# Four source blocks in one weight tile, bounds taken from exponentials, and a re-ranked instruction list in a four-layer graph network

## The chip, the cores and the metric

The kernel runs on one NeuronCore of a Trainium2 chip. The metric is device time in microseconds (us) of one execution, as a median of several executions; less is better. The engines are named as in the profile: PE is TensorE (matmuls), PEld its weight loads, DVE is VectorE, ACT is ScalarE, POOL is GpSimd, SP is SyncE, which here only issues DMAs. L1083 means line 1083 of the kernel before.

## The reference: what is computed

Sixteen graphs (B = 16) of N = 1024 nodes with D = 256 features each pass through four layers. Each layer is `x = x + layer(relu(layernorm(x)), adj)`; `adj` is a symmetric 0/1 matrix with ones on its diagonal.

```
layer 0: relu(h @ W_upd + (adj^T @ (h @ W_msg)) / degree + bias)
layer 1: 4 heads of 64: softmax over neighbours of leaky_relu(e_src_i + e_dst_j, 0.01),
         weighted sum of h @ W, + bias, relu, + h @ W, layernorm over the head's 64 features
layer 2: 4 heads of 64: the same attention with slope 0.2, weighted sum, then elu
layer 3: 1 head of 256: the same attention with slope 0.2, weighted sum
```

## The kernel before, in words

**Mathematics.** Everything is in float32. The exponential of a leaky ReLU of a sum is factored: up to a factor that cancels in the softmax, the weight of source j for target i is `max(exp((1-slope)*s_i), exp(-(1-slope)*e_j)) * mask[j, i]`, and the other factor `exp(e_j)` is multiplied into the features. So one DVE instruction makes the weights of 128 sources: `masked` (L1077 to L1090; the instruction is L1083) takes `max` of a row `r` (the same in all partitions) and a per-partition scalar `tt`, times the mask. PE then multiplies these weights with the features. A guard at the end compares bounds of the exponents (tile `mx`) with a limit; a general program would run if they were exceeded, which these inputs do not bring about.

**Per graph.** `layer0` normalises and transposes `x` (`norm_t`), projects it (L1112 to L1129: split in two float32r parts), and gathers over the adjacency (L1143, L1146; PE alone is busy, 64 pairs of matmuls). `heads` is run for layers 1 and 2: normalise, `project_all` (L984 on PE, L1003 on ACT), `terms`, and then for each of four heads eight source blocks `jb`, each one `masked` of 128x1024 on DVE and one `product` on PE (L1266, 32 records in the trace), and an epilogue mostly on DVE. `layer3` does the same for one head of 256 features in four groups `i2` of 256 targets: eight `masked` of 128x256 and eight `product` (L1420, 4 records each) a group, then a reciprocal (L1434), two final additions (L1445) and the store.

**Terms.** `terms` (L1014) makes for each attention layer: `es` = exp of the source term (ACT, L1024), its transpose (PE, L1034), a copy `r4` to SBUF (ACT, L1038), a write to DRAM (`rd`, L1042) and, by `spread`, a broadcast read into `r` (L1067). `bounds` (DVE, L1050 to L1052) takes three maxima of the raw terms from the projected tile `wh`; after it, because it overwrites these terms, `raise_t` (ACT, L1057 and L1058) makes `tt` and raises the target terms in place. `weigh` (DVE, L1247) or, in layer 3, eight ACT scalings (L1407) then multiply features with the raised terms.

**Buffers.** Every tile has a tag with so many buffers (`BUFS`). Tag `p` has six tiles of 128x1024 float32: each head weight block takes one, each layer-3 weight block takes one too and uses 256 of its 1024 columns, and `r4` takes one as well. Tag `acc` (two PSUM tiles) holds the sums of a head or group.

**What sets the order.** The engines run lists that a planner, class `Plan`, writes at build time. `do` records an operation with its engine, an estimated cost and its dependences, and a priority: the PE time of the graph's earlier operations (`plan.pos`), plus the graph's offset `b * SHIFT` (38.75 us apart), plus a per-stage and per-engine `RANK`, plus `slack`. `emit` repeatedly takes, among all ready operations, the one that can start earliest; ties in that time go to the lower priority number. Each engine executes its list in that order, so an instruction that waits holds what stands behind it on the same engine. A gate keeps the operations of graph b + 2 out of the list until the first operation of layer 3 of graph b, so at most about two graphs are under way.

Of the kernel before, what the change touches and what calls it, by code (L numbers as in the profile page):

```python
# [8 lines left out]
F32 = mybir.dt.float32  # L9
# [9 lines left out]
P = 128  # L19
# [7 lines left out]
SHIFT = 38.75  # L27

ENGINES = ("pe", "dve", "act", "pool", "sp")
RANK = {  # L30
    "load": (-255, -45, -146, -223, -161),
    "setup": (147, 44, -129, 45, 72),
    "norm0": (132, -159, -111, 18, -3),
    "split0": (-94, 119, -51, -165, -111),
    "mask": (77, 143, 41, 193, 218),
    "gather0": (241, -7, 71, 23, 10),
    "norm1": (-60, -62, -162, -146, -99),
    "project1": (20, 26, -5, 26, -6),
    "weights1": (-164, 7, -45, 57, -13),
    "heads1": (-192, -212, -213, -62, -111),  # L40
    "last1": (-26, -102, 9, -196, -80),
    "norm2": (-206, -157, 81, 6, -21),
    "project2": (79, -60, -360, 87, -40),
    "weights2": (94, -3, 153, -153, 12),
    "heads2": (-112, -33, -288, -105, -59),
    "last2": (-21, -230, -230, -36, -82),
    "norm3": (-477, -373, -518, -355, -261),
    "project3": (148, 162, -14, -78, 0),
    "weights3": (170, 143, 167, 44, 87),
    "last3": (43, -259, -75, -14, -59),  # L50
# [4 lines left out]
    "mv": 4, "st": 2, "rstd": 4, "shift": 4, "tt": 3, "es": 2, "dg": 2, "rden": 2, "sth": 1, "mh": 2, "rsh": 2,  # L55
# [16 lines left out]
class Plan:  # L72
# [8 lines left out]
    def __init__(self):  # L81
        self.ops, self.pos, self.gate, self.stage = [], 0.0, None, None

    def do(self, eng, cost, fn, r=(), w=(), lag=0.0, slack=0.0, kind="f", dma=0.0):
# [24 lines left out]
        deps.discard(k)  # L109
        self.ops.append((eng, cost, lag, fn, deps, bufs, self.pos + slack + RANK[self.stage][ENGINES.index(eng)], kind, dma))  # L110
# [3 lines left out]
    def emit(self):  # L114
# [14 lines left out]
        while ready:  # L129
            best = None  # L130
            for k in ready:
# [19 lines left out]
                if at is not None and (best is None or (at, prio, k) < best):  # L151
                    best = (at, prio, k)
            at, _, k = best
# [445 lines left out]
def tile_factored(  # L599
# [56 lines left out]
    mx = const.tile([P, B * 9], F32, name="f_mx")  # L656
    rdn = const.tile([P, B * NB], F32, name="f_rdn")
# [351 lines left out]
    def terms(wh, nh, slope, ecol, scol, k):  # L1009


        tt = buf(small, "tt", [P, NB, nh])
        r4 = buf(work, "p", [P, N])
        rd = buf(dram, "rd", [nh, N])  # L1014

        def ed():
# [3 lines left out]
        es = buf(small, "es", [P, nh, NB])  # L1020
# [4 lines left out]
                es.t, wh.t[:, :, scol : scol + nh].rearrange("p n h -> p h n"), AF.Exp, scale=1.0 - slope  # L1025
            ),
            r=[(wh, ib) for ib in range(NB)],
            w=[es],
# [5 lines left out]
            lambda: nc.tensor.transpose(pt.t[:m, :P], es.t.rearrange("p h n -> p (h n)"), ident),  # L1034
            r=[es],
# [12 lines left out]
        def bounds():  # L1048
            es = wh.t[:, :, scol : scol + nh]
            nc.vector.tensor_reduce(mx[:, k : k + 1], ed(), AX.XY, ALU.max)  # L1050
            nc.vector.tensor_reduce(mx[:, k + 1 : k + 2], ed(), AX.XY, ALU.min, negate=True)
            nc.vector.tensor_reduce(mx[:, k + 2 : k + 3], es, AX.XY, ALU.max)  # L1052

        do("dve", 0.4, bounds, r=[wh])

        def raise_t():
            nc.scalar.activation(tt.t, ed(), AF.Exp, scale=-(1.0 - slope))  # L1057
            nc.scalar.activation(ed(), ed(), AF.Exp)  # L1058

        do("act", 0.5, raise_t, w=[tt, wh])  # L1060
# [14 lines left out]
        return tt, spread  # L1075

    def masked(r, tt, mask, jb, h, lo, hi):  # L1077

        w = buf(work, "p", [P, N])
        do(  # L1080
            "dve",
            (hi - lo + 125) / 960.0,
            lambda: nc.vector.scalar_tensor_tensor(  # L1083
                w.t[:, : hi - lo], r.t[:, lo:hi], tt.t[:, jb, h : h + 1], mask.t[:, jb, lo:hi], op0=ALU.max, op1=ALU.mult
            ),
            r=[r, tt, mask],
            w=[w],
        )
        return w
# [143 lines left out]
    def heads(b, l, xs, mask, w, slope, epilogue, keep):  # L1233
# [19 lines left out]
        for h in range(H):  # L1253
# [22 lines left out]
            epilogue(b, h, ps, wh, xs, 8.0 if h + 1 < H else 0.0)  # L1276
# [19 lines left out]
    def epilogue1(b, h, ps, wh, xs, slack):  # L1296
# [45 lines left out]
        do("pool", 2.0, root, r=[mb], w=[rs], lag=0.9, slack=slack)  # L1342
# [53 lines left out]
    def layer3(b, xs, mask):  # L1396
# [15 lines left out]
        for i2 in range(NB // 2):  # L1412
            plan.stage = "weights3"
            ps = buf(acc_p, "acc", [P, 2, 512])
            for jb in range(NB):
                w = masked(r, tt, mask, jb, 0, i2 * 2 * P, (i2 + 1) * 2 * P)

                def product(w=w, ps=ps, jb=jb):
                    for q in range(2):
                        nc.tensor.matmul(  # L1420
                            ps.t[:, q, : D + 1],
                            w.t[:, q * P : (q + 1) * P],
                            wh.t[:, jb, : D + 1],
                            start=(jb == 0),
                            stop=(jb == NB - 1),
                        )

                do("pe", 0.87, product, r=[w, (wh, jb)], w=[ps])
# [12 lines left out]
            for q in range(2):  # L1441
                do(
                    "dve",
                    0.5,
# [26 lines left out]
    for b in range(B):  # L1471
        plan.pos, plan.gate = b * SHIFT, gates.get(b)
# [17 lines left out]
    for k, (t, most) in enumerate(((tot, 0.0), (mx, TERM_MAX), (rdn, 1e30))):  # L1490
        nc.vector.tensor_scalar(t, t, most, None, op0=ALU.is_le)
        nc.vector.tensor_reduce(m[:, k : k + 1], t, AX.X, ALU.min)
# [58 lines left out]
```

## Time and profile before

| quantity | value |
|---|---|
| median of 3 runs | 2736.85 us (2735.02 to 2740.15) |
| the profiled execution: its time, its span | 2741.27 us, 2739.4 us |
| granted TensorE clock, mean of the span | 0.972 |
| DVE busy | 2357.3 us (86% of the span) |
| ACT busy, POOL busy | 1143.5 us (42%), 878.0 us (32%) |
| POOL's accumulating DMA issue after layer 2's heads waits for DVE (`x L1216 <- DVE y L1388`) | 435.8 us in 46 waits |
| the reciprocal of the last layer-3 group of graphs 0, 13, 14, 15 begins at | 417, 2525, 2633, 2731 us |
| HBM read, written | 228.21 MB, 17.37 MB |

How to read it: "busy" of an engine is the time in which it executes; a row of the groups gives the line, the engine, the operation, the tiles and shapes, the count, the total and mean duration, and the idle time of that engine just ahead of such instructions with what ended it. A wait is read as "who waited for whom: total, times, longest". The windows list, for a stretch of the span, busy time and number of instructions of PE, PEld, DVE, ACT and POOL, then the granted clock, the DMA share and GB/s.

### The profile page before, as it was taken

To read this page: it belongs to the slowest core of one execution; us is meant where nothing else is said; L and a number is where in the kernel's file an instruction comes from. 1 tells how busy PE (TensorE), PEld (TensorE's weight loads), DVE (VectorE), ACT (ScalarE), POOL (GpSimd) and SP (SyncE) were. 2 spreads that over 40 slices of the span, in tenths; PEclk is the share of its full clock that TensorE was granted. 3 is DMA by queue.
4 is the path that set the end of the run, shared out by engine and by line. 5 is a ranking of instruction groups with operands and counts; after the bars stand their busy time and mean duration, and the time that the engine had idled before them with its cause. 6 is when DMAs were issued, how large, how long until landed. Compare 5 with 4: busy or idle time off the path is not lost. (4 is left out here: it accounts for less than half of the span.)

```text
span 2739.4 us, 92386 instructions
## 1 busy us (share of the span) xinstructions
PE 2547.4 (93%) x40667; PEld 2285.7 (83%) x40667; DVE 2357.3 (86%) x4790; ACT 1143.5 (42%) x2753; POOL 878.0 (32%) x907
## 2 busy tenths in 40 slices
PE   7867999999999999999999999999999999999786
PEld 6767798888888888889888889888888988888775
DVE  2699689898988989899898989989898898989884
ACT  4431625344353444525344452534435353453222
POOL 3332234324252332424224251422425133241210
PEclk9989999999999999999999999999999999999998
DMA  8724547356472745547255563735546263562121
GB/s 194 171 44 84 113 87 165 82 128 117 99 143 53 159 91 129 105 91 163 60 144 97 118 125 71 163 75 133 112 107 134 63 158 81 130 118 66 33 52 29
DMA packets 397318, 293.58 MB, mean 107 GB/s; under 512 B 179301, under 2 KB 345706, under 8 KB 396906
## 3 DMA queue, kind: packets, MB, share of 16 engines
q0 software_dynamic: 232992, 92.29, 24.8%
q1 hardware_dynamic: 160752, 193.05, 24.4%
q8 instruction: 321, 5.26, 0.8%
q10 hardware_dynamic: 3162, 2.24, 0.3%
q14 instruction: 91, 0.75, 0.1%
HBM read 228.21 MB, written 17.37 MB: 90 GB/s over the span
## 5 line engine op out<-in xcount | busy, mean ns | idle before, releaser
L1083 DVE SCALAR_TENSOR_TENSOR p<-r,tt,mask 128x1024 f32<-128x1024 f32 (+1 forms) x1536 | 1473.3, 1010 | 109.2 <-PE acc L1266 40.8
L1266 PE MATMUL acc<-wide,p 128*64 128x65 f32 x32768 | 1064.6, 227 | 135.7 <-DVE p L1083 129.3
L1266 PEld LDWEIGHTS acc<-wide,p 128*64 128x64 f32 x32768 | 1017.2, 141 | 204.0 <-issue 99.0
L984 PE MATMUL mm<-f_w,ht 128*128 128x264 f32 (+2 forms) x2048 | 477.0, 387 | 1.4 <-ACT ht L973 1.3
L1420 PE MATMUL acc<-wide,p 128*128 128x257 f32 x2048 | 462.2, 382 | 10.1 <-DVE p L1083 9.9
L1420 PEld LDWEIGHTS acc<-wide,p 128*128 128x128 f32 x2048 | 386.1, 191 | 68.1 <-issue 11.1
L984 PEld LDWEIGHTS mm<-f_w,ht 128*128 128x128 f32 x2048 | 384.6, 192 | 61.2 <-ACT ht L973 3.0
L954 ACT ACTIVATE hn<-x,shift,rstd 128x256 f32<-128x256 f32 x512 | 269.1, 591 | 257.5 <-DVE shift L941 157.1
L1356 ACT ACTIVATE t<-t,mh,rsh 128x64 f32<-128x64 f32 x512 | 176.7, 428 | 198.2 <-DVE mh L1346 174.3
L1143 PE MATMUL mm<-wide,adjr 128*128 128x258 f32 x1024 | 254.5, 289 | 0.0
L1146 PE MATMUL mm<-wide,adjr 128*128 128x256 f32 x1024 | 247.9, 282 | 0.0
L1003 ACT COPY wide<-mm 128x264 f32<-128x264 f32 (+1 forms) x384 | 141.3, 378 | 218.7 <-PE mm L984 216.5
L1216 POOL DMA_DIRECT2D x<-y x48 | 76.6, 1596 | 447.4 <-DVE y L1388 435.8
L934 POOL TENSOR_SCALAR rstd<-mv 128x4 f32<-128x4 f32 x128 | 60.7, 474 | 434.6 <-DVE mv L929 402.3
L1143 PEld LDWEIGHTS mm<-wide,adjr 128*128 128x128 f32 x1024 | 195.9, 191 | 1.7
L1146 PEld LDWEIGHTS mm<-wide,adjr 128*128 128x128 f32 x1024 | 194.2, 190 | 1.5
L922 DVE BATCH_NORM_STATS2 st<-x 128x6 f32<-128x256 f32 x512 | 183.2, 412 | 8.4 <-DMA x<-in_x_dram 5.6
L967 PE MATMUL mm<-f_ident,hn 128*128 128x128 f32 x1024 | 168.0, 300 | 20.2 <-ACT hn L954 17.2
L973 ACT COPY ht<-mm 128x512 f32<-128x512 f32 x256 | 137.8, 580 | 104.9 <-PE mm L967 103.9
L1157 POOL TENSOR_SCALAR dg<-f_deg 128x1 f32<-128x1 f32 x128 | 61.0, 476 | 359.7 <-ACT f_deg L1154 357.4
L967 PEld LDWEIGHTS mm<-f_ident,hn 128*128 128x128 f32 x1024 | 125.2, 151 | 50.4 <-ACT hn L954 35.5
L935 POOL TENSOR_TENSOR rstd<-rstd,f_mhalf 128x4 f32<-128x4 f32 x128 | 162.2, 1268 | 10.7
(103 smaller groups left out, 2179.3 us busy)
## 6 DMA issues: line engine op xcount, KB each, us to landing
r<-rd SPq DMA_DIRECT2D x144, 512.0 KB, 3.9
adjr<-in_adj_dram POOLq DMA_DIRECT2D x128, 512.0 KB, 4.7
nat<-in_adj_dram SPq DMA_DIRECT2D x128, 512.0 KB, 6.6
out_dram<-o SPq DMA_DIRECT2D x64, 256.0 KB, 2.8
x<-in_x_dram SPq DMA_DIRECT2D x31, 512.0 KB, 5.1
x<-t POOLq DMA_DIRECT2D x48, 256.0 KB, 5.5
x<-y POOLq DMA_DIRECT2D x48, 256.0 KB, 4.5
mask<-sq SPq DMA_TRANSPOSE x128, 4.7
```

Source lines behind the costliest of these rows:

```text
L922: lambda st=st, ib=ib, k=k: nc.vector.bn_stats(st.t[:, k, :], xs.t[:, ib, :]),
L935: nc.gpsimd.tensor_tensor(rstd.t, rstd.t, mhalf[:, :nh], op=ALU.pow)
L954: nc.scalar.activation(hn.t[:, k, :], xs.t[:, hf * nh + q, :], AF.Relu, bias=shift.t[:, q : q + 1], scale=rstd.t[:, q : q + 1],)
L967: nc.tensor.transpose(pt.t[:, k, c, :], hn.t[:, k, c * P : (c + 1) * P], ident)
L984: nc.tensor.matmul(out, ht.t[:, c, ib * P : (ib + 1) * P], w.t[:, c, lo:hi], start=(c == 0 and k == 0), stop=(c == KC - 1), skip_group_che ...
L1003: lambda ib=ib, ps=ps: nc.scalar.copy(wh.t[:, ib, :cols], ps.t[:, :cols]),
L1083: lambda: nc.vector.scalar_tensor_tensor(w.t[:, : hi - lo], r.t[:, lo:hi], tt.t[:, jb, h : h + 1], mask.t[:, jb, lo:hi], op0=ALU.max, op1= ...
L1143: nc.tensor.matmul(ps.t[:, : D + 2], a.t[:, ib, :], hi.t[:, ib, : D + 2], start=(ib == 0), stop=False)
L1146: nc.tensor.matmul(ps.t[:, :D], a.t[:, ib, :], lo.t[:, ib, :D], start=False, stop=(ib == NB - 1))
L1266: nc.tensor.matmul(ps.t[c : c + 64, g, q * E1 : (q + 1) * E1], p.t[:, i2 * 64 : (i2 + 1) * 64], xw.t[:, jb, h * E1 : (h + 1) * E1], start= ...
L1356: nc.scalar.activation(t.t[:, ib, :], t.t[:, ib, :], AF.Identity, bias=mb.t[:, 3, ib : ib + 1], scale=rs.t[:, ib : ib + 1],)
L1420: nc.tensor.matmul(ps.t[:, q, : D + 1], w.t[:, q * P : (q + 1) * P], wh.t[:, jb, : D + 1], start=(jb == 0), stop=(jb == NB - 1),)
```

## The change

1. Layer 3's weights of four source blocks share one tile of tag `p`: block `q = jb % 4` goes to columns 256q to 256q + 255, and a new tile is taken only for q = 0. The instruction's size stays 128x256, and the products read their part.
2. `es` and `tt` become one tile `et` (row 0 the source exponentials, row 1 the target ones); `r4` gets a small buffer of its own instead of one of tag `p`. `raise_t` is recorded ahead of `bounds`. `bounds` is now two reductions, of `et` and of the raised target terms, recorded after `raise_t` with a slack of 19.714; the limits are exponentials of the old limit, kept in a tile `lim` that six POOL memsets fill, and compared by one `tensor_tensor` at the end.
3. All `masked` of a graph keep their order (`row="weights"`: each depends on the one before).
4. The planner: after it has found the operation that can start earliest, it takes a better-ranked one of the same engine if that can start within `HOLD` (PE 0.1, DVE 0.25, ACT 0.45 us, POOL and SP 0). Each graph's offset is `b * 147.75 + START[b]` in place of `b * 38.75`. All `RANK` numbers are new; the slack of the first three heads' epilogues goes from 8 to 23; the estimated cost of the head norm's root goes from 2.0 (lag 0.9) to 2.6 (lag 1.2) and of the final addition from 0.5 to 0.43.

```diff
-SHIFT = 38.75
+SHIFT = 147.75
+HOLD = (0.1, 0.25, 0.45, 0.0, 0.0)
+START = (-50, 120, 90, 96, 162, 174, 157, 173, 171, 159, 102, 27, 24, -31, -99, -188)
...
-    "weights1": (-164, 7, -45, 57, -13),
+    "weights1": (-159, 14, 48, 187, 22),
...
-    "weights2": (94, -3, 153, -153, 12),
+    "weights2": (-69, -102, -110, -395, -48),
...
-    "project3": (148, 162, -14, -78, 0),
-    "weights3": (170, 143, 167, 44, 87),
-    "last3": (43, -259, -75, -14, -59),
+    "project3": (460, 307, 133, 13, 73),
+    "weights3": (381, 312, 355, -1, 200),
+    "last3": (-85, -237, -117, -157, -144),
...
+        if row is not None:
+            if row in self.rows:
+                deps.add(self.rows[row])
+            self.rows[row] = k
...
+            until = at + HOLD[ENGINES.index(self.ops[k][0])]
+            for a, p, q in could:
+                if self.ops[q][0] == self.ops[k][0] and a <= until and p < prio:
+                    at, prio, k = a, p, q
...
-        tt = buf(small, "tt", [P, NB, nh])
-        r4 = buf(work, "p", [P, N])
+        et = buf(small, "et", [P, 2, nh, NB])
+        r4 = buf(small, "r4", [P, P])
...
+        def raise_t():
+            nc.scalar.activation(et.t[:, 1], ed().rearrange("p n h -> p h n"), AF.Exp, scale=-(1.0 - slope))
+            nc.scalar.activation(ed(), ed(), AF.Exp)
+
+        do("act", 0.5, raise_t, w=[(et, 1), wh])
+
         def bounds():
-            es = wh.t[:, :, scol : scol + nh]
-            nc.vector.tensor_reduce(mx[:, k : k + 1], ed(), AX.XY, ALU.max)
-            nc.vector.tensor_reduce(mx[:, k + 1 : k + 2], ed(), AX.XY, ALU.min, negate=True)
-            nc.vector.tensor_reduce(mx[:, k + 2 : k + 3], es, AX.XY, ALU.max)
-
-        do("dve", 0.4, bounds, r=[wh])
-
-        def raise_t():
-            nc.scalar.activation(tt.t, ed(), AF.Exp, scale=-(1.0 - slope))
-            nc.scalar.activation(ed(), ed(), AF.Exp)
-
-        do("act", 0.5, raise_t, w=[tt, wh])
+            nc.vector.tensor_reduce(mx[:, k : k + 2], et.t.rearrange("p s h n -> p s (h n)"), AX.X, ALU.max)
+            nc.vector.tensor_reduce(mx[:, k + 2 : k + 3], ed(), AX.XY, ALU.max)
+
+        do("dve", 0.45, bounds, r=[et, wh], slack=19.714)
...
-        w = buf(work, "p", [P, N])
+        w = w or buf(work, "p", [P, N])
+        c = q * (hi - lo)
...
-            epilogue(b, h, ps, wh, xs, 8.0 if h + 1 < H else 0.0)
+            epilogue(b, h, ps, wh, xs, 23.0 if h + 1 < H else 0.0)
...
-                w = masked(r, tt, mask, jb, 0, i2 * 2 * P, (i2 + 1) * 2 * P)
+                q = jb % 4
+                w = masked(r, tt, mask, jb, 0, i2 * 2 * P, (i2 + 1) * 2 * P, w if q else None, q)
...
-        plan.pos, plan.gate = b * SHIFT, gates.get(b)
+        plan.rows = {}
+        plan.pos, plan.gate = b * SHIFT + START[b], gates.get(b)
```

## The prediction

> **What bounds the kernel now.** I read the busy shares, then the groups, the waits, the windows by stage, and last the timeline around the gaps of PE.
>
> ```profile
> PE 2547.4 (93%) x40667; PEld 2285.7 (83%) x40667; DVE 2357.3 (86%) x4790; ACT 1143.5 (42%) x2753; POOL 878.0 (32%) x907
> ...
> PEclk9989999999999999999999999999999999999998
> ...
> L1083 DVE SCALAR_TENSOR_TENSOR p<-r,tt,mask 128x1024 f32<-128x1024 f32 (+1 forms) x1536 | 1473.3, 1010 | 109.2 <-PE acc L1266 40.8
> L1266 PE MATMUL acc<-wide,p 128*64 128x65 f32 x32768 | 1064.6, 227 | 135.7 <-DVE p L1083 129.3
> ```
>
> PE is busy 93%, and what ends most of its idle time (129.3 of some 192 us) is DVE's weights. The change leaves PE's work as it is, so a gain can only come from PE's idle time and from the clock that is withdrawn around it. DVE, at 2357.3/16 = 147.3 us a graph, comes next.
>
> ```profile
> 110.00:313.00 203.00, 152.97 (x3271) 137.99 (x3270) 181.78 (x346) 68.14 (x167) 57.78 (x44) 0.90 0.35 70
> 313.00:417.00 104.00, 102.89 (x1415) 91.99 (x1415) 84.06 (x160) 41.55 (x100) 30.48 (x35) 1.00 0.58 120
> 417.00:2525.00 2108.00, 2034.63 (x33007) 1830.82 (x33007) 1905.12 (x3862) 926.90 (x2236) 720.25 (x728) 0.98 0.53 112
> 2525.00:2633.00 108.00, 88.57 (x1260) 79.63 (x1262) 88.17 (x195) 34.46 (x88) 22.19 (x18) 0.89 0.21 49
> 2633.00:2674.00 41.00, 35.57 (x1022) 31.81 (x1016) 39.76 (x40) 3.78 (x6) 4.72 (x3) 1.00 0.29 41
> 2674.00:2701.00 27.00, 12.49 (x55) 9.38 (x51) 7.51 (x31) 14.30 (x34) 2.53 (x4) 0.75 0.06 20
> ```
>
> Three regimes. The ramp (110 to 313 us): both first graphs are in their heads, DVE is the bound (181.78 of 203), PE lacks 50 us and the clock is 0.90, which costs about 153 x 0.10 = 15 us more: 65 us. The steady part: the last layer-3 groups of graphs 0 and 13 lie 2108 us apart, 2108/13 = 162.2 us a graph, with PE busy 2034.6/13 = 156.5. The end: 19.4 + 5.4 + 14.5 us without matmuls, then layer 3 of the last graph alone.
>
> Where do 5.7 us of PE's time go in each steady graph? One gap makes most of it, here in one graph (from the timeline: start and length in us, engine, line, tiles, count, and in brackets the idle time before it and who ended it; the last line is a window as above); 4.1 us recur in each graph:
>
> ```profile
> 1380.68 0.87 DVE L1083 SCALAR_TENSOR_TENSOR p<-r,tt,mask 128x256 f32<-128x256 f32 x2
> ...
> 1383.05 1.66 DVE L1083 SCALAR_TENSOR_TENSOR p<-r,tt,mask 128x256 f32<-128x256 f32 x4
> ...
> 1382.21 5.37 PE L1420 MATMUL acc<-wide,p 128*128 128x257 f32 x24
> ...
> 1391.70 2.00 PE L1266 MATMUL acc<-wide,p 128*64 128x65 f32 x32 [4.12 <-DVE p L1083]
> ...
> 1393.00:1398.00 5.00, 5.00 (x79) 4.55 (x77) 5.00 (x5) 3.04 (x6) 0.38 (x1) 0.57 1.05 338
> ```
>
> DVE lays in 2 + 4 = 6 layer-3 blocks, exactly the six tiles of tag `p`. PE eats them (24 records, 4 each) by 1387.6 while DVE is in an elu, an addition, norm statistics and layer-3 outputs, and then stands for 4.12 us. Afterwards the clock is 0.68 over 4 us and 0.57 over 5 us: with 1.3 and 5.0 us of PE work in them that is 0.4 + 2.15 = 2.5 us more. So the gap costs 6.6 us of 162.2.
>
> **What the Trainium skill says.** "TensorE: Matmul & The Clock Gate", the part on the HAM clock gate: after about 3.4 us of idling PE's clock is halved until about 3.4 us of work have passed. The trace agrees (0.57 after a gap of 4.12 us). The same page, on engine queue depths, has ACT and DVE as strict FIFOs; the waits below agree. "Perfetto Trace Analysis", Optimization Strategy: the same gap repeating on the engine that should be saturated can mean too few buffers for the next tile. The six blocks before that gap fit this.
>
> ```profile
> PE acc L1266 <- DVE p L1083: 129.3, 56, 8.5
> DVE f_mx L1050 <- ACT wide L1003: 111.1, 21, 11.5
> DVE p L1083 <- PE acc L1420: 35.3, 79, 4.9
> ACT wide L1058 <- DVE f_mx L1052: 30.4, 14, 2.3
> ```
>
> **The change, part by part.**
>
> *One tile for four layer-3 blocks.* The instructions and their sizes stay: 512 of 477 ns. Six tiles now hold 24 such blocks, or eight blocks (a whole group) hold two tiles and leave four to the heads. It removes the 35.3 us of DVE behind L1420, and lets DVE lay in more for PE: another six blocks are 6 x 4 x 0.226 = 5.4 us of PE work (5.37 / 24 = 0.224 a record), above the gap of 4.12. Bounds: 0 if the new list does not lay in more ahead of that stretch, 13 x 6.6 = 86 us if every gap closes. A tile is now held until its fourth product; with two tiles a group against six before I cost that at nothing, since the heads' weights gain tiles; if PE lets a quarter-used tile lie, its price is one tile of six, one head block of 1.2 us of DVE lead. `r4` outside tag `p` frees one tile from L1038 to the write of `rd` (about 2 us), 48 times; it is inside the same bound. I take half of the gap's cost, 3.5 us a graph: **13 x 3.5 = 45 us**. I chose half because the list must still place the blocks well and DVE's 147 us a graph leave little room in 156.
>
> *Bounds from exponentials.* Before: 32 x (207 + 202 + 175) + 16 x (160 + 154 + 154) ns = 18.7 + 7.5 = 26.2 us of DVE. After, two reductions: for 64 elements I estimate 0.25 us (207 ns at 32 elements, 160 at 8: 2 ns an element, so 0.21 to 0.27), and the last one stays: 32 x 0.43 + 16 x 0.32 = 18.9. So 7 us less of DVE in all, 0.5 us a graph, nothing where PE is the bound. The 111.1 us that DVE stood before L1050 are mostly under PE's projections and would be waited out at the next instruction; I count 0. L1058's 30.4 us go; what is late next is `r` (`rd` 1.7 us and the broadcast 3.7 us after it), so again 0; bounds 0 to 30/16 = 1.9 us a graph, in the half above. The new waits: in layer 2 `weigh` writes over what `bounds` reads and stands behind it on DVE itself; in layer 3 the planner puts the ACT scalings after `bounds`. Behind these scalings on ACT stand copies of projections and norms, and PE's L1420 waits for them. `bounds` has a slack of 19.7, so this may be late (rival D). Six POOL memsets at the start (0.1 us each, as L1100's 106 ns) lie before PE's first matmul at 13.7 us, which waits for a DMA: 0, or 0.6 us if uncovered. The last comparison replaces one of like width: 0 to 0.1 us.
>
> *Weights in order.* Same engine, so no wait is added; the order inside a graph was nearly this: 0, at worst a few blocks of 1.2 us in a graph.
>
> *Offsets and ranks.* At the start graph 0 now stands 318 us ahead of graph 1 in the priorities (-50 against 147.75 + 120), not 38.75. Before, the two layers 0 shared PE and DMA until 110 us, with DVE busy 31.9 of 110 us; the first head weights came at 110.1. If graph 0 goes first it needs half of that PE work (about 52 us a graph by L1143, L1146, L1182 and the projections), and can begin its heads some 20 us earlier; graph 1's layer 0 then fills PE under graph 0's heads, and graph 2 gets past its gate, the first layer-3 operation of graph 0, well before 313 us. Moved with it are graph 1's adjacency loads on POOL's queue and its mask loads and transposes on SP's: later, and behind graph 0's, whose DMA share (above 1 from 60 to 110 us) is eased. Of the 65 us I take **30**; bounds 0 and 55. At the end offsets are 80 and 59 apart, and layer 3's PE rank of 381 against -69 for layer 2's weights keeps layer 3 back as filler. Some of 39.4 us of gaps and about 16 of clock (88.6 x 0.11 + 12.5 x 0.25 + 29.8 x 0.1) can be had; I take **8**, bounds -10 (more serial) and 25.
>
> *Holds.* The list may leave DVE up to 0.25 us idle, ACT 0.45. If one in twenty of some 2600 DVE operations is held, 130 x 0.25 = 32 us of DVE, 2 a graph, under its slack of 162.2 - 147.3 = 15; 0 for PE, 4 us if all of the ramp's share is exposed. Gain where it closes a gap: in the half above.
>
> **Sum.** The profiled execution took 2741.3 us (span 2739.4 and 1.9 around it). 2741.3 - 45 - 30 - 8 = 2658. It lies 4.4 us above the median of the runs, so 2658 - 4.4 = **2654**.
>
> **Rivals.**
> - A, the forecast (2615 to 2690): half of the steady gap, half of the ramp. 0.48.
> - B, nearly all gaps close: 86 + 55 + 20 = 161, so 2741.3 - 161 - 4.4 = 2576. For: six blocks run out in every graph. Against: DVE at 147 of 156 us. 0.14.
> - C, only ramp and end gain, because DVE, not the tiles, is short in the steady part and the gap moves: 2741.3 - 38 - 4.4 = 2699. For: DVE is busy 2.97 of 3 us in the gap. 0.24. Its neighbour, no part of the list works out on the chip (the change doesn't do what it says): 2737, within 0.2%. 0.04.
> - D, slower: `bounds`, late by its slack, holds layer 3's scalings, and PE runs out of filler once more in each graph: 16 x 6.6 = 106, against A's ramp and end of 38: 2741.3 + 106 - 38 - 4.4 = 2805. It decides from 38 / 16 = 2.4 us of new PE idling a graph upward. Against: PE has other graphs' work. 0.10.
>
> **Range.** 0.2% (5.5 us) is about what a measurement of this kernel can tell from no change. Left out are D and the unchanged case (0.14), a sliver of C, and the deep half of B (0.05): 2585 to 2728. Faster 0.86, same 0.04, slower 0.10.
>
> **What would show it.** Right: graphs 0 to 13 less than 159 us apart; DVE waiting for L1420's successor near 0; the gap before L1266 under 3.4 us and the clock above 0.98; first head weights before 100 us; PE idle from 110 to 313 us below 30 us. Wrong: ACT's scalings waiting for `bounds` by more than 2 us a graph (D); unchanged 162 us a graph with DVE busy through the gap (C); a tail longer than 65 us after the last head's epilogue.

## The result, and the profile after

| | before | after |
|---|---|---|
| median (lowest to highest, 8 runs each) | 2738.53 us (2735.02 to 2742.44) | 2749.7 us (2745.03 to 2752.47) |
| ratio | 1 | 1.0038, 95% interval 1.0027 to 1.0049 |
| the profiled execution: its time, its span | 2741.27, 2739.4 us | 2745.03, 2743.2 us |
| PE busy, idle between matmuls, clock | 2547.4, 192, 0.972 | 2594.0, 149, 0.989 |
| DVE busy | 2357.3 | 2364.7 |
| DVE behind head products; behind layer-3 products | 40.8 (29 times); 35.3 (79) | 69.6 (133); 45.7 (42) |
| PE's changes between head products and other work | 352 | 806 |

The change makes the kernel 0.4% slower; the forecast was a time 3% shorter. The two profiled executions lie 3.8 us apart, the medians 11.2, so what follows from the traces accounts for the difference of these two executions and not for all of the 11.2. (The last row is counted in the records of the matmuls. A head product has 64 columns; all other work of PE is called full-width here.) The page of the kernel after, the lines that answer to the first ones shown of before:

```profile
PE 2594.0 (95%) x40667; PEld 2257.6 (82%) x40667; DVE 2364.7 (86%) x4742; ACT 1146.2 (42%) x2753; POOL 854.8 (31%) x913
...
PEclk9989999999999999999999999999999999999998
...
L1101 DVE SCALAR_TENSOR_TENSOR p<-r,et,mask 128x1024 f32<-128x1024 f32 (+1 forms) x1536 | 1473.6, 1011 | 129.7 <-PE acc L1290 69.6
...
L1290 PE MATMUL acc<-wide,p 128*64 128x65 f32 x32768 | 1087.1, 225 | 75.9 <-DVE p L1101 51.6
```

L1101 and L1290 are the old L1083 and L1266. PE's idle time ahead of head products has fallen from 135.7 to 75.9 us, as forecast, but the same matmuls are busy 22.5 us longer, and DVE stands longer ahead of its weights (109.2 before, 129.7 now). The gap that the prediction was built on is gone. At the place of the one that it showed, the timeline of after (same columns) has:

```profile
1389.15 5.47 PE L1446 MATMUL acc<-wide,p 128*128 128x257 f32 x24
...
1392.42 2.45 DVE L1101 SCALAR_TENSOR_TENSOR p<-r,et,mask 128x1024 f32<-128x1024 f32 x2
...
1394.55 2.09 PE L1290 MATMUL acc<-wide,p 128*64 128x65 f32 x64
```

Six layer-3 blocks end at 1394.6 and the head products follow at once. By stage (the windows; columns as before):

```profile
110.00:313.00 203.00, 165.06 (x3221) 146.15 (x3218) 181.63 (x362) 82.31 (x199) 70.73 (x63) 0.94 0.58 104
...
408.00:2378.00 1970.00, 1925.25 (x30478) 1675.73 (x30479) 1769.15 (x3531) 857.64 (x2064) 647.03 (x673) 1.00 0.57 111
2378.00:2621.00 243.00, 218.50 (x3631) 191.46 (x3628) 217.90 (x454) 105.83 (x260) 72.87 (x70) 0.96 0.41 80
2621.00:2743.20 122.20, 102.85 (x1331) 87.72 (x1329) 77.51 (x146) 17.91 (x40) 7.25 (x7) 0.94 0.20 49
```

The last layer-3 reciprocal of graph 0 comes at 408 us (417 before), that of graph 12 at 2378 (2364 before). So the ramp gives 9 us, the twelve graphs between cost 1970 - 1947 = 23, and the end gives 375 - 365 = 10: 4 us more in all, the difference of the two spans. **The loss is in the steady part**, where PE now runs at full clock. For a like stretch of eleven graphs, from the end of graph 1 to that of graph 12, before and then after:

```profile
579.00:2364.00 1785.00, 1722.71 (x27929) 1550.12 (x27929) 1611.77 (x3267) 784.30 (x1892) 610.49 (x617) 0.98 0.53 112
```

```profile
573.00:2378.00 1805.00, 1764.62 (x27939) 1536.19 (x27940) 1621.65 (x3237) 786.17 (x1892) 593.39 (x617) 1.00 0.57 111
```

A steady graph takes 1785/11 = 162.3 us before and 164.1 after. PE's idle time goes from 5.7 to 3.7 us a graph, its busy time from 156.6 to 160.4. DVE's busy time goes from 146.5 to 147.4, its idle time from 15.7 to 16.7. DVE's waits in that stretch, before and after:

```profile
DVE f_mx L1050 <- ACT wide L1003: 56.0, 11, 5.1
DVE p L1083 <- PE acc L1266: 35.0, 22, 3.0
DVE t L1369 <- ACT t L1356: 22.4, 11, 2.0
DVE p L1083 <- PE acc L1420: 16.3, 44, 0.4
DVE mh L1346 <- POOL rsh L1340: 11.7, 33, 0.4
DVE p L1083 <- ACT tt L1057: 10.1, 11, 0.9
```

```profile
DVE p L1101 <- PE acc L1290: 56.2, 109, 1.5
DVE f_mx L1073 <- ACT et L1067: 52.0, 10, 5.5
DVE p L1101 <- PE acc L1446: 34.0, 33, 1.8
DVE t L1393 <- ACT t L1380: 11.9, 10, 2.8
```

The waits for ACT and POOL (`t`, `mh`, `tt`) shrank by some 32 us; the waits for PE's products grew by 39.

### The profile page after: what moved, and what is told of

It reads as the page before. It is cut to its first block, busy times and chain, and to the rows that moved or that the text cites. A ratio compares the mean times of both kernels' runs of the same rounds, so it can differ in the third digit from the quotient of the medians.

```text
span 2743.2 us, 92362 instructions
## 1 busy us (share of the span) xinstructions
PE 2594.0 (95%) x40667; PEld 2257.6 (82%) x40667; DVE 2364.7 (86%) x4742; ACT 1146.2 (42%) x2753; POOL 854.8 (31%) x913
## 5 line engine op out<-in xcount | busy, mean ns | idle before, releaser
L1101 DVE SCALAR_TENSOR_TENSOR p<-r,et,mask 128x1024 f32<-128x1024 f32 (+1 forms) x1536 | 1473.6, 1011 | 129.7 <-PE acc L1290 69.6
L1290 PEld LDWEIGHTS acc<-wide,p 128*64 128x64 f32 x32768 | 1014.7, 139 | 210.7 <-issue 111.6
L1290 PE MATMUL acc<-wide,p 128*64 128x65 f32 x32768 | 1087.1, 225 | 75.9 <-DVE p L1101 51.6
L1003 PE MATMUL mm<-f_w,ht 128*128 128x264 f32 (+2 forms) x2048 | 502.6, 392 | 7.2 <-ACT ht L992 7.1
L1446 PE MATMUL acc<-wide,p 128*128 128x257 f32 x2048 | 481.8, 387 | 11.6 <-DVE p L1101 11.6
L1003 PEld LDWEIGHTS mm<-f_w,ht 128*128 128x128 f32 x2048 | 374.7, 191 | 70.4 <-ACT ht L992 12.9
L1405 ACT ACTIVATE y<-t 128x512 f32<-128x512 f32 x64 | 40.4, 631 | 573.6 <-DVE t L1310 573.6
L986 PE MATMUL mm<-f_ident,hn 128*128 128x128 f32 x1024 | 161.2, 285 | 32.3 <-ACT hn L973 25.4
L915 ACT ACTIVATE sq<-nat 128x1024 uint8<-128x1024 int32 x128 | 135.9, 1062 | 100.2 <-DMA mask<-sq 91.4
L954 POOL TENSOR_TENSOR rstd<-rstd,f_mhalf 128x4 f32<-128x4 f32 x128 | 174.2, 1361 | 10.7
L986 PEld LDWEIGHTS mm<-f_ident,hn 128*128 128x128 f32 x1024 | 113.1, 142 | 64.1 <-ACT hn L973 45.6
```

The lines of the kernel that those rows point to most:

```text
L954: nc.gpsimd.tensor_tensor(rstd.t, rstd.t, mhalf[:, :nh], op=ALU.pow)
L986: nc.tensor.transpose(pt.t[:, k, c, :], hn.t[:, k, c * P : (c + 1) * P], ident)
L1003: nc.tensor.matmul(out, ht.t[:, c, ib * P : (ib + 1) * P], w.t[:, c, lo:hi], start=(c == 0 and k == 0), stop=(c == KC - 1), skip_group_che ...
L1101: lambda: nc.vector.scalar_tensor_tensor(w.t[:, c : c + hi - lo], r.t[:, lo:hi], tt.t[:, 1, h, jb : jb + 1], mask.t[:, jb, lo:hi], op0=ALU ...
L1290: nc.tensor.matmul(ps.t[c : c + 64, g, q * E1 : (q + 1) * E1], p.t[:, i2 * 64 : (i2 + 1) * 64], xw.t[:, jb, h * E1 : (h + 1) * E1], start= ...
L1446: nc.tensor.matmul(ps.t[:, k, : D + 1], w.t[:, c : c + P], wh.t[:, jb, : D + 1], start=(jb == 0), stop=(jb == NB - 1),)
```

## The experiments

In the kernels that leave work out, and in those that edit the finished list, the planner makes its list first, and the edit comes after that; so the list is that of before or of after, as the text says. "After" is 2749.7 us throughout; the median of "before" measured beside the others was 2739 to 2742, and every ratio is to that.

**What PE's order costs.** My first theory was that PE's changes between head products and full-width products are the loss. Two runs undo and imitate them: in after, full-width work goes ahead of up to three head products, which brings the list's changes from 935 to 819; in before, the middle two of "full, full, head, head" change places, 430 to 744 changes (both counted in the list, with the changes inside layer 0's float32r work too, so that after's 806 are 935 here and before's 352 are 430).

```diff
+            if ops[pe[i]][7] == "f" and 0 < n < 4 and i + 1 + n < len(pe) and ops[pe[i + 1 + n]][7] == "f":
+                ys, z = pe[i + 1 : i + 1 + n], pe[i + 1 + n]
+                slow = max(late.get(y, 0.0) for y in ys) + ops[z][1]
+                new = self.inputs(z, ys[0], order, begun, done) if slow <= most else None
```

> The changed kernel, the lists of DVE, ACT, POOL and SP as they are; on PE alone, where one full-width operation, up to three head products and another full-width operation follow each other and the second full-width one already has its inputs, it goes ahead of the head products (which are put off by at most 1 us). PE's list then changes between head products and other matmuls 819 times instead of 935. Theory S (PE is the bound, and each such change costs it about 0.157 us: the last step of a head run 0.152 instead of 0.03, the first and last of a full-width run 0.32 and 0.31 instead of 0.217): 116 x 0.157 = 18 us less, about 2732. Theory W (the changed kernel loses by waits on DVE and ACT, not on PE's order): within 4 us of 2750, or slower because head products come later.

Measured: 2792.86 us, ratio 1.0203 (1.0188 to 1.0217), 43 us more than after. Theory S misses; of theory W the second half ("slower because head products come later") fits.

```diff
+            if "".join(self.ops[k][7] for k in pe[i - 1 : i + 3]) in ("ffcc", "ccff"):
+                new = self.inputs(pe[i + 1], pe[i], order, begun, done)
```

> The kernel before, the lists of DVE, ACT, POOL and SP as they are; on PE alone, where two full-width operations meet two head products (or the other way round), the middle two change places if the inputs are there. Changes between head products and other matmuls in PE's list: 744 instead of 430. Theory S: 314 x 0.157 = 49 us more, about 2787. Theory W: PE's order costs nothing by itself, within 8 us of 2738.

Measured: 2767.0 us, ratio 1.0097 (1.0082 to 1.0113), 28 us more than before, between the two forecasts (49, and at most 8). More changes cost something in before, though this run can't tell their own price from the delay of what was put off. Fewer of them cost more in after: a head product put off by one full-width product comes late for DVE. The grouped kernel's waits (engine, line, waited for: total, times, longest):

```profile
DVE p L1164 <- PE acc L1353: 103.5, 91, 2.4
...
PE acc L1353 <- DVE p L1164: 82.0, 112, 5.6
```

Each engine now waits more for the other (69.6 and 51.6 in after).

Two further edits of after's order, the other way round, put a single full-width product behind the next one to three head products, where those could begin within 0.9 or 0.6 us.

```diff
+                ready = max([done[d] + self.WAIT[ops[d][0]] for d in ops[pe[i + 1]][4] if ops[d][0] != "pe"], default=0.0)
+                if ready <= begun[y] + spare:
```

> The changed kernel with its lists, except on PE: where a single operation of layer 3's products, the gather, layer 0's split or layer 1's projection stands between head products, it goes behind the next one to three head products if these could begin at most 0.9 us after it (PE may idle up to that; what needs the moved operation follows it). Changes between head products and other matmuls: 758 in the list instead of 935. It is the mirror of the first run, which also lowered that number but put the head products off. Theory C (the period is set by the loop of DVE's head weights and PE's head products; other matmuls have time): 10 to 40 us less than 2750, with DVE's wait for head products below 69.6 us. Theory P (PE's time, edges included): 177 x 0.09 = 16 us less from the edges, against up to 40 us of new idling: between 2734 and 2775, and PE's idle time up.

> As the run before it, with at most 0.6 us in place of 0.9 (786 changes). Theory C: between the changed kernel and the run before it. Theory P: 149 x 0.09 = 13 us less, against up to 22 us of new idling: between 2737 and 2759.

Measured: 2831.0 us, ratio 1.033 (1.0316 to 1.0344), and 2819.37 us, ratio 1.0295 (1.0280 to 1.0311), above the ranges of both theories: misses. So no local edit of after's order that I tried does without its changes.

**The price of a change by itself.** Behind the kernel before, PE alone on resident tiles:

```diff
+        for i in range(64):
+            for j in range(1):
+                for i2 in range(16):
+                    c = i2 % 2 * 64
+                    nc.tensor.matmul(hs[c : c + 64, 0, :E1], pw[:, i2 * 64 : (i2 + 1) * 64], wd[:, 0, :E1], start=True, stop=True)
+            for j in range(1):
+                for q in range(2):
+                    nc.tensor.matmul(fs[:, q, : D + 1], pw[:, q * P : (q + 1) * P], wd[:, 1, : D + 1], start=True, stop=True)
```

> The kernel before, and behind it PE alone on resident tiles, so that PE waits for nothing: 64 head products (16 matmuls of 64 columns each) and 64 layer-3 products (2 matmuls of 128x257), first in 4 x (16 heads, 16 layer-3), 8 changes; then 64 x (one, one), 128 changes; then 32 x (two heads, one layer-3), which leaves out half of the layer-3 products, 64 changes; then the first once more. Theory I (a change of PE between the two kinds has a price of its own, some 0.09 us as the second experiment suggests): the second stretch is 120 x 0.09 = 10 to 11 us longer than the first. Theory II (the long edge steps are waits for inputs): the second stretch is as long as the first within 2 us.

Measured in one execution, in its windows (first, second, third, fourth stretch):

```profile
2734.20:2852.30 118.10, 118.08 (x2304) 109.88 (x2304) 0.58 (x3) 0.00 (x0) 0.00 (x0) 0.99 0.01 2
2852.30:2989.70 137.40, 137.40 (x2306) 108.25 (x2306) 0.00 (x0) 0.00 (x0) 0.00 (x0) 1.00 0.01 2
2989.70:3088.20 98.50, 98.50 (x2177) 83.96 (x2176) 0.00 (x0) 0.00 (x0) 0.00 (x0) 1.00 0.01 3
3088.20:3205.00 116.80, 116.80 (x2307) 108.45 (x2306) 0.21 (x2) 0.00 (x0) 0.00 (x0) 1.00 0.01 3
```

The same 2304 records take 137.4 us mixed and 117.45 (mean of the first and fourth) grouped: 19.95/120 = **0.166 us a change**; the third stretch gives (98.5 - 117.45 + 128 x 0.217)/56 = 0.158. PE is busy all the while and waits for nothing. The price is real, and nearly twice what the second experiment let me expect.

In the steady eleven graphs the changes between head products and other work go from 263 to 606, 31 a graph more: 31 x 0.166 = 5.2 us a graph, as an estimate. It takes the price of a change to layer-3 products for all of them. Some 154 of the new changes are of that kind, and some 129 are to projections, which show nearly the same steps in the trace of after (0.326 us for the first record of a run next to a head product, 0.316 for the last, 0.217 inside); the rest were not priced.

PE's busy time grew by 3.8 us a graph. This is net of the clock: by its records in the trace, the reduced clock took some 2.3 us of PE's busy time from each of these graphs in before (mean 0.98) and nothing in after (1.00). So PE's work at full clock grew by about 6 us a graph. The changes can be most of that; about 1 us stays unexplained.

**Where the changes come from.** The planner charges PE 0.09 us for a change from a full-width to a head product, and the new hold lets it take a better-ranked operation that starts up to 0.1 us later. With the hold at 0.05, the list has 114 changes (both directions) in its first 4500 entries, and 394 with 0.1. With 0.05 from start to end the planner finds no free buffer on its way and makes no whole list; with 0.05 in the first 2500 entries it does:

```diff
-            until = at + HOLD[ENGINES.index(self.ops[k][0])]
+            few = self.ops[k][0] == "pe" and n - done.count(None) < 2500
+            until = at + (0.05 if few else HOLD[ENGINES.index(self.ops[k][0])])
```

> The kernel after in full; one number of its planner is other for the first 2500 of some 8900 list entries (the first four to five graphs): PE's hold is 0.05 in place of 0.1 us, which is below the 0.09 us that the planner charges PE for a change from a full-width product to a head product, so the planner no longer takes a better-ranked head product at the price of a change. The list's changes of PE between head products and other work fall from 806 to 670. Theory M (the changes are what after pays and its order needs none of them): 136 x 0.15 = 20 us of PE's time less, the graphs that begin in that part less than 163 us apart (164.7 in after), 2732 to 2745 in all. Rival N (the changes are the price of handing over between DVE and PE in time, as in the first and the eleventh experiment): the early graphs 166 to 175 us apart, with DVE or PE waiting more, 2765 to 2810 in all, and the later graphs as in after.

Measured: 2800.63 us, ratio 1.0214 (1.0197 to 1.0231). Graphs 0 to 4 end their layer 3 at 357, 557, 720, 944 and 1119 us (408, 573, 737, 901, 1066 in after); from then on they are 165 us apart as in after. Graphs 1 to 4 take 200, 163, 224 and 175 us. At the end of graph 2 this kernel is 17 us ahead of after, and graphs 3 and 4 lose 70. The whole time lies in theory N's range (2765 to 2810), the single graphs fit neither theory. Fewer changes came with a worse order; but graph 3 lies near the place where the hold is switched, so the size of this loss is that of this one list, and the run doesn't show what the smaller hold would give throughout.

**The tile of four blocks alone.** In before, list unchanged:

```diff
+            def shared():
+                if not four:
+                    four.append(make())
+                return four[0]
...
+                four = four if q else []
+                w = masked(r, tt, mask, jb, 0, i2 * 2 * P, (i2 + 1) * 2 * P, four, q)
```

> The kernel before with its lists unchanged, the layer-3 weights of four source blocks laid into one tile. The prediction's step (too few tiles make the gap of 4.1 us in each graph): DVE's 35 us before layer 3's weights go; if the buffers alone make the gap, 13 x 6.6 = 86 us less. Theory S, and the reading that the gap lies in DVE's order and in the row that the next head needs: within 5 us of 2738, the gap of 4 us still there.

Measured: 2765.82 us, ratio 1.0098 (1.0083 to 1.0113), 26 us more, where the forecasts were 86 less or no change beyond 5. Its waits:

```profile
DVE p L1124 <- PE acc L1307: 83.4, 43, 5.0
...
PE acc L1307 <- DVE p L1124: 135.8, 70, 8.5
```

DVE's weights no longer wait for layer-3 products (35.3 us in before), though the reciprocal at the end of a group now does (32.9 us; 4.7 in before). And the tile that is not given back until its fourth product is now lacking for the heads: DVE waits 83.4 us for head products (40.8 in before), and PE's gap stays (135.8 against 129.3). A list made for six separate blocks gains nothing from the sharing by itself. Since DVE's list stands as it was, DVE could not lay in more blocks here, so the run doesn't test what the roomier tiles give to a list that uses them.

**Bounds left out** (the maxima of the exponent terms are not computed; all else as in after).

```diff
-            nc.vector.tensor_reduce(mx[:, k : k + 2], et.t.rearrange("p s h n -> p s (h n)"), AX.X, ALU.max)
-            nc.vector.tensor_reduce(mx[:, k + 2 : k + 3], ed(), AX.XY, ALU.max)
+            pass
```

> The changed kernel with the same lists, the two reductions of the bounds left out (the guard then always sees zero for them). Theory S: DVE only waits there under work of PE; 0 to 7 us less. Theory W, by way of the bounds (late by their slack, ahead of layer 3's scalings; DVE stands 95 us before them): 20 us less or more than that.

Measured: 2749.9 us, ratio 1.0040 (1.0027 to 1.0054), the time of after, as theory S had it. DVE's wait moves to its next instruction:

```profile
DVE wide L1302 <- ACT wide L1100: 104.3, 17, 13.4
```

So neither the bounds nor their new place is the loss; rival D of the prediction falls.

**Closing the gap of before by hand.** In before, layer 1's row of terms (transpose, copy, write, two broadcasts) is put sooner in 14 graphs; then, in addition, the first three layer-1 weight blocks go ahead of layer 3's norm statistics on DVE.

```diff
+            hoist(t)
+            c = next(k for k in uses[t] if ops[k][0] == "act")
+            hoist(c)
+            rd = next(k for k in uses[c] if ops[k][0] == "sp")
+            hoist(rd)
```

> The kernel before with its lists, except that in 14 graphs layer 1's source row is made sooner: its transpose on PE goes ahead of the run of head products in front of it (6.6 us by the list), and the copy, the write and the two broadcasts follow at once. DVE's list stays. Theory G (the gap of 4.1 us comes from this row being late: the broadcast was issued 2 us after the transpose, and the first head weights could not start before about 1388): DVE's order still has the statistics of layer 3 in front of those weights, so the gap stays and the time is within 6 us of 2738. Theory T (too few tiles): no change either.

> As the run before it, and on DVE the first three weight blocks of layer 1 go ahead of the layer-3 statistics that stood in front of them (3.6 us). The number of changes between head products and other matmuls is nearly the kernel before's (430 in the list), so nothing is given back on PE. Theory G: the gap closes and the clock is not withdrawn behind it: 13 x (4.1 + 2.5) = 86 us at most; about half, because the statistics, and with them layer 3's projection, come 3.6 us later: 2695, range 2655 to 2725. Theory T (too few tiles, or DVE is the bound there and a gap moves elsewhere): within 6 us of 2738.

Measured: 2746.04 us, ratio 1.0022 (1.0012 to 1.0032), and 2779.04 us, ratio 1.0142 (1.0123 to 1.0162). The first is as forecast (5.7 us above the before measured beside it); the second lies outside the ranges of both theories (2655 to 2725; within 6 us of 2738). In it PE's gap before the heads shrinks and another opens:

```profile
PE mm L1057 <- ACT hn L1044: 99.6, 29, 7.8
PE acc L1356 <- DVE p L1173: 76.2, 46, 8.5
```

PE waits 76.2 us for weights (129.3 in before), but 99.6 us for the normalised features of layer 3 (17 in before), whose statistics DVE now does later. Taking the gap away at one place of DVE's list put it at another.

**Which engine's work sets the time.** Six kernels with unchanged lists leave work out: "less DVE" leaves out the 12 row operations a graph for bias, gamma and beta of layer 1; "less PE" leaves out the low part of layer 0's gather; "half heads" leaves out half of the targets in the head products of source blocks 1 to 6.

```diff
-                lambda v=v, op=op: nc.vector.tensor_tensor(t.t, t.t, row(v), op=op),
+                lambda: None,
...
-                    nc.tensor.matmul(ps.t[:, :D], a.t[:, ib, :], lo.t[:, ib, :D], start=False, stop=(ib == NB - 1))
...
-                    for i2 in range(2 * NB):
+                    for i2 in range(NB * (jb % 2 if 0 < jb < NB - 1 else 0), NB * (jb % 2 + 1 if 0 < jb < NB - 1 else 2)):
```

> The changed kernel with its lists, twelve DVE instructions of 0.69 us a graph left out: the products and sums with layer 1's bias, gamma and beta rows (8.3 us a graph, 132 us in all). Theory P (PE is the bound in the steady part, as the prediction had it): 0 to 25 us less. Theory C (the period is a chain that runs through both engines, each nearly full): 60 to 110 us less.

> The changed kernel with its lists, the low part of layer 0's gather left out on PE (64 matmuls of 0.12 us a graph: 7.7 us, 123 us in all; the output loses the low bits of the messages). Theory P: 90 to 123 us less. Theory C: 40 to 90 us less.

> The kernel before with its lists, the same twelve DVE instructions a graph left out (132 us in all). Theory P: 0 to 25 us less. Theory C: 60 to 110 us less, and not less than in the changed kernel.

> The kernel before with its lists, the low part of layer 0's gather left out on PE (123 us in all). Theory P: 90 to 123 us less. Theory C: 40 to 90 us less. If the changed kernel loses by PE's edges, it gains more from this than the kernel before.

> The list of the kernel after unchanged; of the head products of source blocks 1 to 6 one half of the targets is left out (even blocks the second half, odd blocks the first), so PE has some 768 x 0.49 = 375 us less to do, all in the head products that DVE's weights feed; DVE's work is the same. Theory H (the hand-over between DVE's head weights and PE's head products sets the pace, and any later product delays DVE by way of the six tiles): 60 to 150 us less, since DVE's 69.6 us of waits for head products go and PE's fillers come sooner. Theory W (PE's work is not the limit at all, as when 123 us of the gathers were taken away): within 15 us of the kernel after. If PE were the bound: more than 250 us less.

> The same left out with the list of the kernel before. Theory H: 30 to 110 us less (DVE's waits for head products there are 40.8 us), and less is gained than with the list of after. Theory W: within 15 us of the kernel before. If PE were the bound: more than 250 us less.

The last two put both larger cuts together:

> The list of after unchanged; left out are the 12 row operations a graph of DVE (bias, gamma, beta; 132 us) and half of the head products of source blocks 1 to 6 on PE (375 us), the two cuts that alone gave 32 and 40 us less. Theory T (after has two limits at nearly the same time, PE's work with its many changes and DVE's work with its waits, so that each cut alone runs into the other): more than the sum, 90 to 140 us less than after, 2610 to 2660; DVE's 63 us behind the head products' end in the steady graphs are nearly gone. Rival K (a chain of latencies through one graph sets the time, neither engine's work): no more than the larger of the two, 30 to 50 us less, about 2705.

> The same two cuts with the list of before, where they gave 55 us less and 18 us more alone. Theory T (before is DVE's work with its waits, PE has room): 55 to 90 us less than before, 2650 to 2685, since DVE's waits behind the products shrink a little. Rival K: no more than 55 us less, with DVE's waits for ACT grown by what its own work lost.

| left out | us of work, estimated | before: time, ratio (interval) | after: time, ratio to before (interval) |
|---|---|---|---|
| DVE row operations | 132 | 2685.88, 0.980 (0.9784 to 0.9816) | 2717.5, 0.9906 (0.9889 to 0.9924) |
| part of PE's gathers | 123 | 2730.03, 0.9954 (0.9937 to 0.997) | 2749.09, 1.0027 (1.0019 to 1.0034) |
| half of PE's head products | 375 | 2758.42, 1.0065 (1.0049 to 1.0081) | 2709.43, 0.988 (0.986 to 0.99) |
| DVE row operations and half of the head products | 507 | 2636.59, 0.9609 (0.9591 to 0.9627) | 2643.04, 0.9639 (0.9623 to 0.9655) |

The busy times of the pages fell by less than these estimates: DVE's by 119 us in before and 125 in after for its row operations, PE's by 94 and 60 for the gathers, and by 216 and 233 for the head products, where the clock fell too. None of the first six times lies in a range of either of its theories, so the reading that follows was made after them, and the last two runs are its test.

The steady eleven graphs of four of them (before: less DVE, half heads; after: less DVE, half heads):

```profile
567.00:2320.00 1753.00, 1703.45 (x27929) 1549.18 (x27929) 1530.99 (x3137) 783.27 (x1892) 591.21 (x617) 0.98 0.54 114
```

```profile
575.00:2370.00 1795.00, 1576.26 (x19481) 1379.48 (x19481) 1615.01 (x3271) 787.89 (x1892) 615.83 (x617) 0.93 0.52 111
```

```profile
569.00:2355.00 1786.00, 1755.37 (x27941) 1535.63 (x27943) 1535.32 (x3105) 785.39 (x1893) 584.02 (x617) 1.00 0.58 112
```

```profile
569.00:2344.00 1775.00, 1593.42 (x19474) 1319.74 (x19471) 1612.12 (x3234) 785.90 (x1892) 598.32 (x617) 0.98 0.58 112
```

Divided by 11 these give two limits for each list, estimates good to about 1 us, since PE's work is cut in one place only and the clock falls with it (0.93 in the second line). With PE relieved a graph takes what DVE's list takes with the waits that stay: 163.2 us in before (146.8 busy, 16.4 waiting), 161.4 in after (146.6 and 14.8). Some of these waits are still for PE's projections, which the cut leaves whole. With DVE relieved it takes nearly what PE's list takes: 159.4 in before (PE busy 154.9), 162.4 in after (159.6, PE idle 2.8), where DVE now stands for the end of a head in the less-DVE kernel of after:

```profile
DVE rden L1340 <- PE acc L1321: 63.1, 36, 3.8
```

In before, DVE's limit (163) lies above PE's (159), and the full kernel takes 162.3. In after the order has lowered DVE's limit by 1.8 and raised PE's by 3.0; they now lie within 1 us of each other, and the full kernel takes 164.1, above both. On these estimates PE's limit of 162.4 would by itself give the time of before, and the loss of 1.8 us a graph is nearly all in the 1.7 above it. That this is the two engines waiting for each other fits the waits shown above, but no run shows it alone.

Together the cuts give more than the sum of each alone: in after 107 us (forecast 90 to 140) against 32 + 40, in before 105 (forecast 55 to 90) against 55 - 18. The steady eleven graphs, after and then before:

```profile
550.00:2284.00 1734.00, 1570.60 (x19497) 1306.17 (x19495) 1526.95 (x3106) 782.33 (x1893) 596.79 (x617) 1.00 0.59 115
```

```profile
558.00:2275.00 1717.00, 1533.96 (x19481) 1348.32 (x19481) 1527.87 (x3139) 785.19 (x1892) 607.11 (x618) 0.96 0.54 116
```

A graph takes 157.6 us in after and 156.1 in before. With PE relieved, cutting DVE's work by 7.9 us a graph gains 7.1 in before (163.2 to 156.1): there DVE's own work sets nearly all of the time. In after a cut of 7.8 gains 3.8 (161.4 to 157.6), and DVE's waits grow from 14.8 to 18.8. So two limits close together explain much, and a chain of latencies that no engine's work moves (rival K) can't be the whole; but in after waits still eat half of the cut.

What the two limits don't say is why the cut in the gathers gives nothing in after and 11 us in before: that work lies in another place of the graph than the heads, and which places of a graph count wasn't tried further.

## Why the prediction was wrong

**What bounds the kernel** is the step that failed. It read PE's 93% as the bound and PE's idle time as what can be had; DVE's 15 us a graph it called slack. The runs show the reverse for before: without half of the head products PE is busy 216 us less and nothing is gained (ratio 1.0065), and without its row operations DVE is busy 119 us less and 55 are gained. DVE's 15.7 idle us a graph were no slack, since 16.4 stay when PE is relieved; PE's 5.7 were, in that list.

**The steady gap, 45 us.** The mechanism came about: the gap closed, the clock went to 1.00, PE's idle time fell by 2.0 us a graph. The price was not in the sum. It said that the instructions and their sizes stay and so PE's work too; but PE's busy time grew by 3.8 us a graph, and by about 6 without the clock's return. Single head products now stand between full-width ones, 31 changes a graph more at some 0.166 us each, which is most of it. The price stood in the code (the planner charges 0.09 to 0.12 us for a change to or from head products) and I did not read it. So 3.5 us a graph of gain were 1.8 of loss.

**The tile**, held until its fourth product, was costed at nothing: in before's list it costs 26 us by itself (fourth experiment). DVE's waits behind layer-3 products, which were to vanish, are 45.7 us, fewer but longer. The Trainium skill's "Perfetto Trace Analysis", Optimization Strategy, was cited for reading a repeated gap as too few buffers; the six blocks fitted that, but the page says only that it can be so, and with the shared tiles alone the gap stayed (135.8 us against 129.3). Whether the new list could close it without them was not tried.

**The ramp, 30 us**, was mis-sized: 9. First head weights came at 98.9 us, as forecast before 100, and PE was idle 37.9 us in the window to 313 against forecast 30. But DVE is as busy there as before (181.6 us): with graph 0 alone ahead it stands 12.9 us for one layer's terms (L1073), after 12.2 us for the raised terms of the layer before (L1271, which multiplies them into the features) that end at 79.6 us, ahead of this window.

**The end, 8 us**, was right in size: 10, of which 9 are less idle time of PE there (53.0 to 43.8 us).

**The bounds at about 0** were right: they cost DVE 18.6 us against 18.9 forecast, and leaving them out changes nothing. (DVE's whole busy time, forecast 7 us less, is 7.4 more; what that is was not followed up.) The time came out on the slower side, as rival D had it, but not by D's mechanism. Rival C named DVE as what is short in the steady part, which the runs bear out for before; but its gap was to stay, and it closed. **Holds** were given DVE's idle time as a price and nothing on PE; by the planner's lists the hold on PE is where the changes come from.

Open: whether the new order without its changes would be faster, and how much ranks, offsets and holds each add to it. Most lists with one of them undone leave the planner without a free buffer, so that apart from the partial hold they were not tried on the chip.

## What to carry to other kernels

Before an idle gap is counted as gain, relieve the engine that has it (leave out some of its work, order unchanged) and see whether the time moves; a busy share of 93% beside one of 86% did not tell here which of the two is the limit, since both run fixed lists that wait for each other. Nor does busy time plus waits, which fills the stretch on every engine; what tells is how much of an engine's waiting stays when the other has less to do. Read the clock of the relieved run beside its time, and relieve both engines once. An order that hands over in smaller pieces pays for each change of kind, so count the changes and multiply.

## What was not expected of the hardware

In the run of PE alone, a change between 64-column and 128-column matmuls costs time with all inputs resident. From the start of one record to the next: inside a run of head products 0.030 us, the last of a run 0.152; inside a run of layer-3 products 0.217, the first 0.321 and the last 0.310, then 0.007 for the first head record. One round of both changes costs 0.122 + 0.104 + 0.093 - 0.023 = 0.296 us by these steps, 0.33 by the length of the stretches. All of it is in the busy time of PE, not in its idle time. And PE relieved of work lost clock: with half of the head products the steady clock of before's list was 0.93, where it was 0.98 with all of them, and PE's share of that stretch was 88% in place of 97%.
